# A sampling round's weighted sums, and what follows them, stand one round later in program order

## The chip, the cores and the metric

The kernel runs on one core of a Trainium2 chip. The metric is the device time of one execution in microseconds (us); the median of three executions before the change is 7738.43 us. All arithmetic is in float32.

## The reference

The input is four images of 256 channels by 64 by 64 pixels. Each image goes through four layers in a row. The first one is the one that the change touches, cut here to that part:

```python
# L0, per image: y = leaky_relu(bn(conv1x1(normed x))); xp = inproj(y)
offset, mask = linear(depthwise3x3(y))            # 4 groups x 9 points per pixel
sg   = reference_grid + dilation_grid + offset    # where each point lies
samp = grid_sample(pad(xp), sg)                   # 4 neighbours, bilinear
dout = (samp * softmax(mask)).sum(points)         # 36 weighted points per pixel
x2   = bn(y + outproj(dout))
x2   = x2 * squeeze_excite(mean(x2))              # needs the whole image's mean
out  = y + fc2(leaky_relu(fc1(x2)))
# then L1 linear attention with 5x5 depthwise, L2 3x3 convolution with signed
# weights, L3 a non-local block with softmax; group norms stand between them
```

The sampling is a gather: every pixel needs 36 points of a table, at addresses that the data decide.

## The kernel before

**Sampling.** `sample(n, ssum)` (L556) samples image n in 293 rounds. A round covers 14 pixels (`RP`), which is 126 of the 128 partitions with 9 points each. Sixteen rounds make a block of 224 pixels; an image has 18 such blocks and one of five rounds. In a round:

- `gathered` (L596) issues four indirect DMAs on GpSimd's queue, one per group, into a tile `g` of which seven buffers exist (L598), and then eight small matmuls on TensorE (L607, "the sums") that multiply the gathered rows by the weights `wm` and add them into `acc`, a PSUM bank used in two halves of two rounds each. Two rounds (`UR`) make a unit.
- `weigh` (L585, VectorE, L591) prepares `wm` for four rounds (`WR`) at a time; two `wm` buffers exist.
- What follows a unit's sums is put into `later`, a table from round number to functions: `moved` (L610, ScalarE copies `acc` to `at`, L612), `turned` (L614, TensorE transposes `at` into `dp`, L617), `spread` (L619, ScalarE copies `dp` into the block's `dT`, L632; of `dT` one buffer exists). After a block's last unit come, for each half of the output channels, `project` (L636, TensorE, L640), `add` (L642, VectorE, L644) and `finish` (L646, ScalarE, L649). At the start of each round, what `later` holds for it is issued (L658).
- `load` (L572) fetches the next block's table addresses and weights into `sl`, from the first round of a block.

**Side work.** The sampling loop is a generator. After each round, `beside` (L1194) advances the programs that run beside it by a portion of their steps: beside image 0 it is the first convolution of the other images and the sampling coordinates; beside image n it is the feed-forward of image n-1, then the linear attention of image n-1, and layers 2 and 3 of image n-2. After image 3's sampling a stretch without sampling finishes the last images.

**Order.** Under `manual_schedule`, TensorE, VectorE, ScalarE and GpSimd execute in the order in which the program issues their instructions. Only the Sync engine's DMA queue is arranged by the framework. GpSimd has, while the sampling goes on, nothing but gathers. So the place of a sampling step is its place among the portions of side work on its own engine:

```python
for f in later.pop(i, ()): f()      # start of round i
...gathered(sl, wm, acc, r)...      # four gathers, eight matmuls
yield 1                             # beside() issues portion i of the side work
```

Before the change, TensorE's order is thus: later(i), sums(i), portion(i), later(i+1), sums(i+1), portion(i+1), and so on.

Of the kernel before, what the change touches and what calls it, by code (L numbers as in the profile page):

```python
# [17 lines left out]
P = 128  # L18
N, C, H, W = 4, 256, 64, 64
HW = H * W  # L20
KT = C // P
# [8 lines left out]
RP, WR, UR, BR = 14, 4, 2, 16  # L30
RS, BP = RP * PT, RP * BR
BLOCKS = [(p0, min(BP, HW - p0)) for p0 in range(0, HW, BP)]
OB = 16
TY, TX = H + 2, W + 3
LEADS = 12, 14, 16, 18
SLOPE = 0.01

# [34 lines left out]
class Net:  # L72
# [483 lines left out]
    def sample(self, n, ssum):  # L556

        nc, sp = self.nc, self.sp
        table = self.tab[n].rearrange("g y x s c -> (g y x) (s c)")
        blocks, images, at, dp, dT, po, later = {}, {}, {}, {}, {}, {}, {}

        def halves(name):

            t = self.ps1.tile([P, 2, 256], F32, name=name, tag=name)
            return cycle([t[:, 0], t[:, 1]])

        accs, dps = halves("acc"), halves("dp")  # L570

        def load(b):  # L572
            p0, np_ = BLOCKS[b]
            whole, part = np_ // RP, np_ % RP

            nr = whole + (part > 0)
            sl = sp.tile([P, BR, G * 5], F32, name="sl")
            rows = self.s_d[n][p0 * PT:p0 * PT + nr * RS, :].rearrange("(r p) f -> p r f", p=RS)
            more = self.s_d[n][p0 * PT + RS:p0 * PT + (nr + 1) * RS, :].rearrange("(r p) f -> p r f", p=RS)
            nc.sync.dma_start(sl[0:RS, 0:nr], rows)  # L580
            nc.sync.dma_start(sl[RS:P, 0:nr], more[0:P - RS])
            rounds = [(r, RP) for r in range(whole)] + [(whole, part)] * (part > 0)
            blocks[b] = sl, rounds

        def weigh(b, r):  # L585

            sl, rounds = blocks[b]
            nu = min(WR, len(rounds) - r)
            wm = self.gp.tile([P, WR, 4 * G, OB], F32, name="wm")
            sh = [P, nu, 4 * G, OB]  # L590
            nc.vector.tensor_tensor(  # L591
                wm[:, 0:nu], self.con("own").unsqueeze(1).unsqueeze(1).to_broadcast(sh),
                sl[:, r:r + nu, G:].unsqueeze(3).to_broadcast(sh), ALU.mult)
            return wm

        def gathered(sl, wm, acc, r):  # L596
            r4, acc = r % WR, acc[:, r % UR * P:(r % UR + 1) * P]
            g = self.gp.tile([P, G, 256], F32, name="g", bufs=7)  # L598
            for i in range(G):
                nc.gpsimd.indirect_dma_start(  # L600
                    out=g[:, i, :], out_offset=None, in_=table,
                    in_offset=bass.IndirectOffsetOnAxis(ap=sl.bitcast(I32)[:, r, i:i + 1], axis=0))


            for x in range(2):
                for i in range(G):
                    nc.tensor.matmul(acc[32 * i:32 * i + 32, :], wm[:, r4, 4 * i + 2 * x:4 * i + 2 * x + 2, :],  # L607
                                     g[:, i, x * P:(x + 1) * P], start=x == 0, stop=x == 1)

        def moved(acc, nu, u):  # L610
            at[u] = sp.tile([P, UR, P], F32, name="at")
            nc.scalar.copy(at[u].rearrange("p v c -> p (v c)")[:, 0:nu * P], acc[:, 0:nu * P])  # L612

        def turned(nu, u):  # L614
            dp[u] = next(dps).rearrange("p (v g s o) -> p v g s o", v=UR, g=G, s=2)
            for v in range(nu):
                nc.tensor.transpose(dp[u][:, v].rearrange("p g s o -> p (g s o)"), at[u][:, v], self.ident)  # L617

        def spread(unit, b, u):  # L619

            if b not in dT:
                p0, np_ = BLOCKS[b]
                dT[b] = sp.tile([P, G, BP], F32, name="dT", bufs=1)
                images[b] = sp.tile([P, KT, BP], F32, name="yb")
                nc.sync.dma_start(images[b][:, :, 0:np_], self.y_d[n][:, :, p0:p0 + np_])
            full = sum(1 for _, m in unit if m == RP)
            for v0, v1, m in ((0, full, RP), (full, len(unit), unit[-1][1])):
                for s in range(2):
                    if v0 < v1:
                        hs = slice(64 * s, 64 * s + 64)  # L630
                        q0 = RP * (unit[0][0] + v0)
                        nc.scalar.copy(  # L632
                            dT[b][hs, :, q0:q0 + m * (v1 - v0)].rearrange("p g (v o) -> p g v o", o=m),
                            dp[u][hs, v0:v1, :, s, 0:m].rearrange("p v g o -> p g v o"))

        def project(b, m):  # L636
            np_ = BLOCKS[b][1]
            po[m] = self.ps("po")
            for k in range(G):
                nc.tensor.matmul(po[m][:, 0:np_], self.ow[:, k, m * P:(m + 1) * P], dT[b][:, k, 0:np_], start=k == 0, stop=k == G - 1)  # L640

        def add(b, m):  # L642
            ym = images[b][:, m, 0:BLOCKS[b][1]]
            nc.vector.tensor_tensor(ym, po[m][:, 0:BLOCKS[b][1]], ym, ALU.add)  # L644

        def finish(b, m):  # L646
            p0, np_ = BLOCKS[b]
            ym = images[b][:, m, 0:np_]
            nc.scalar.activation(ym, ym, AF.Identity, bias=self.sh[:, 4 + m:5 + m],  # L649
                                 scale=self.inv[:, 4 + m:5 + m], accum_out=ssum[:, m, b:b + 1])  # L650
            if m == KT - 1:
                nc.sync.dma_start(self.x2_d[n][:, :, p0:p0 + np_], images[b][:, :, 0:np_])

        load(0)
        order = [(b, r) for b, (_, np_) in enumerate(BLOCKS) for r in range(-(-np_ // RP))]
        wm = weigh(0, 0)
        for i, (b, r) in enumerate(order):
            for f in later.pop(i, ()):  # L658
                f()
            sl, rounds = blocks[b]  # L660
            if r % UR == 0:
                acc = next(accs)
            gathered(sl, wm, acc, r)
            if r == 0 and b + 1 < len(BLOCKS):
                load(b + 1)
            ends = r + 1 == len(rounds)
            if r % WR == 0:
                if r + WR < len(rounds):
                    nxt = weigh(b, r + WR)
                elif b + 1 < len(BLOCKS):  # L670
                    nxt = weigh(b + 1, 0)
            if r % UR == UR - 1 or ends:
                unit = rounds[r - r % UR:r + 1]
                todo = [partial(moved, acc, len(unit), i), partial(turned, len(unit), i), partial(spread, unit, b, i)]

                todo = [(i + 1 + j + (j == 2 and r < UR), f) for j, f in enumerate(todo)]
                if ends:
                    todo += [(i + 4 + m + j, partial(f, b, m)) for m in range(KT) for j, f in enumerate((project, add, finish))]
                for j, f in todo:
                    later.setdefault(j, []).append(f)  # L680
            if r % WR == WR - 1 or ends:
                wm = nxt
            yield 1
        for i in sorted(later):
            for f in later[i]:
                f()
# [73 lines left out]
    def layer1(self, n, st, st2):  # L760
# [3 lines left out]
        with tc.tile_pool(name=f"la{n}", bufs=1, side="right") as sp, \  # L764
# [17 lines left out]
            def step(cost, chains=False):  # L782
# [6 lines left out]
                if chains:  # L789
                    if count % 8 == 6 if self.alone else count in LEADS:  # L790
                        next(made, None)
# [551 lines left out]
```

## Time and profile before

| | |
|---|---|
| three executions | 7737.99, 7738.43, 7746.72 us |
| profiled execution, first to last instruction (the only time that its record gives) | 8805.8 us |
| first gather starts, last gather starts | 134.1 us, 7306.6 us |
| from there to the end | about 1,498 us |
| GpSimd: gathers, mean of one | 4,688, 985 ns |
| TensorE busy, granted clock, over the whole span | 68%, 0.81 |
| VectorE, ScalarE, GpSimd busy | 59%, 25%, 59% |

The profile is of one execution, which took 8805.8 us from its first to its last instruction; that is 13.8% more than the median of the three that were timed without a profile. It is read by stage: the sampling from 134 to 7,308 us, and the stretch without sampling after it. In the rows, "A <- B" names the tile that an instruction writes and the tiles that it reads; the last column is the time for which the engine stood idle before such instructions, and what ended most of that idle time. "issue" is time in which the engine waited for nothing that the profile shows, "remote" is a wait whose releaser the profile could not name.

### The profile page before, as it was taken

Reading aid. Unit: us, or ns where it says so; the run is one execution under the profiler, and the core shown is the slowest. Engines: PE = TensorE matmul, PEld = TensorE weight load, DVE = VectorE, ACT = ScalarE, POOL = GpSimd, SP = SyncE. Lnnn points to the kernel's source line nnn. Section 1 sums busy time; section 2 is a strip of 40 time slices with the busy share of each in tenths; the row PEclk is TensorE's granted clock in tenths of the full one; section 3 lists DMA queues with packets and bytes.
Section 4 is the critical chain, followed back from the end, with each engine's and each line's share of the span. In section 5 each row is a group of like instructions: output and inputs, shape, how many; then the busy total and the mean of one; then the engine's idle time right before and its main releaser. Section 6 shows DMA issues by size and latency. Waiting matters only on the chain. (4 is left out here: it accounts for less than half of the span.)

```text
span 8805.8 us, 95736 instructions
## 1 busy us (share of the span) xinstructions
PE 5993.9 (68%) x36532; PEld 3575.6 (41%) x36532; DVE 5173.3 (59%) x6409; ACT 2183.8 (25%) x4899; POOL 5152.4 (59%) x4950
## 2 busy tenths in 40 slices
PE   4454554448744446688876677888766778986899
PEld 2222222224323322244544443345544433664477
DVE  5444443443466667424777776227777772599834
ACT  1111111112211112122223222222222222465524
POOL 2666666566666666666666656666666661376410
PEclk7676766669866667799988888898878888998999
DMA  6454454444433334444443344444434343220131
GB/s 172 127 155 124 141 154 118 125 145 145 153 105 105 110 105 129 127 130 138 134 135 110 112 121 136 142 134 132 136 115 117 114 118 99 69 74 29 48 98 53
DMA packets 759050, 1042.27 MB, mean 118 GB/s; under 512 B 362432, under 2 KB 472128, under 8 KB 757056
## 3 DMA queue, kind: packets, MB, share of 16 engines
q0 software_dynamic: 225024, 614.77, 24.3%
q1 hardware_dynamic: 533568, 421.39, 16.4%
q8 instruction: 289, 4.73, 0.2%
q14 instruction: 169, 1.38, 0.0%
HBM read 867.08 MB, written 168.69 MB: 118 GB/s over the span
## 5 line engine op out<-in xcount | busy, mean ns | idle before, releaser
L600 POOL DMA_INDIRECT g<-tab,sl x4688 | 4618.5, 985 | 2687.8 <-issue 1224.2
L178 DVE SCALAR_TENSOR_TENSOR agg<-pad,vec,agg 128x1024 f32<-128x1024 f32 x2280 | 2933.5, 1287 | 61.9
L607 PE MATMUL acc<-g,wm 128*32 128x128 f32 x18752 | 1034.8, 333 | 1907.8 <-ACT at L612 1273.7
L607 PEld LDWEIGHTS acc<-g,wm 128*32 128x32 f32 x18752 | 566.8, 128 | 2411.7 <-ACT at L612 1446.1
L1048 PE MATMUL ps<-xd,w 128*128 128x256 f32 x3072 | 752.7, 396 | 51.3 <-issue 37.8
L591 DVE TENSOR_TENSOR wm<-con,sl 128x1024 f32<-128x1024 f32 (+1 forms) x296 | 357.7, 1209 | 711.9 <-remote 533.5
L1048 PEld LDWEIGHTS ps<-xd,w 128*128 128x128 f32 x3072 | 595.1, 199 | 175.0 <-issue 86.0
L632 ACT COPY dT<-dp 64x112 f32<-64x112 f32 x1176 | 285.9, 243 | 1043.7 <-remote 544.3
L742 PE MATMUL ps<-x2f,f 128*128 128x512 f32 x1024 | 499.2, 636 | 19.1 <-issue 7.7
L817 PE MATMUL ps<-xr,qw 128*128 128x512 f32 x768 | 472.0, 746 | 22.1 <-issue 11.1
L727 DVE SCALAR_TENSOR_TENSOR hm<-ps,vec,lk 128x512 f32<-128x512 f32 x256 | 190.8, 750 | 492.9 <-ACT lk L744 405.5
L752 PE MATMUL ps<-hm,f 128*128 128x512 f32 x1024 | 467.1, 605 | 0.9 <-DVE hm L727 0.9
L612 ACT COPY at<-acc 128x256 f32<-128x256 f32 (+1 forms) x588 | 218.3, 371 | 986.3 <-remote 753.2
L999 POOL TENSOR_TENSOR xd<-xp 128x640 f32<-128x640 f32 x64 | 79.4, 1268 | 492.6 <-ACT xp L1011 298.3
L640 PE MATMUL po<-dT,ow 128*128 128x224 f32 (+1 forms) x1216 | 326.1, 419 | 45.4 <-issue 19.3
L617 PE MATMUL dp<-ident,at 128*128 128x128 f32 x1172 | 284.1, 330 | 106.6 <-ACT dT L632 61.0
L865 ACT COPY kt<-pt 128x512 f32<-128x512 f32 x256 | 149.4, 584 | 829.3 <-remote 403.8
L744 ACT ACTIVATE lk<-ps,low 128x512 f32<-128x512 f32 x256 | 174.0, 687 | 666.0 <-PE ps L742 512.1
L1147 PE MATMUL s<-ph,th 128*128 128x512 f32 x512 | 290.2, 672 | 62.5 <-ACT kt L865 15.9
L640 PEld LDWEIGHTS po<-dT,ow 128*128 128x128 f32 x1216 | 265.5, 233 | 113.8 <-issue 68.9
L1167 PEld LDWEIGHTS ps<-gt,pT 128*128 128x128 f32 x2048 | 276.0, 213 | 70.8 <-issue 46.1
L194 POOL TENSOR_TENSOR ak<-ak,m 128x1024 f32<-128x1024 f32 x96 | 228.1, 2376 | 130.6 <-ACT m L193 126.7
(243 smaller groups left out, 8022.0 us busy)
## 6 DMA issues: line engine op xcount, KB each, us to landing
g<-tab,sl POOLq DMA_INDIRECT x4688
x<-x SPq DMA_DIRECT2D x128, 512.0 KB
xr<-x SPq DMA_DIRECT2D x96, 512.0 KB
tab<-xo SPq DMA_DIRECT2D x192, 128.0 KB
x<-in_x SPq DMA_DIRECT2D x32, 512.0 KB
y<-yc SPq DMA_DIRECT2D x32, 512.0 KB
x2f<-x SPq DMA_DIRECT2D x32, 512.0 KB
xyf<-x SPq DMA_DIRECT2D x32, 512.0 KB
```

What stands on the lines that cost most here:

```text
L178: nc.vector.scalar_tensor_tensor(to, s, wt, acc, ALU.mult, ALU.add)
L591: nc.vector.tensor_tensor(wm[:, 0:nu], self.con("own").unsqueeze(1).unsqueeze(1).to_broadcast(sh), sl[:, r:r + nu, G:].unsqueeze(3).to_bro ...
L600: nc.gpsimd.indirect_dma_start(out=g[:, i, :], out_offset=None, in_=table, in_offset=bass.IndirectOffsetOnAxis(ap=sl.bitcast(I32)[:, r, i: ...
L607: nc.tensor.matmul(acc[32 * i:32 * i + 32, :], wm[:, r4, 4 * i + 2 * x:4 * i + 2 * x + 2, :], g[:, i, x * P:(x + 1) * P], start=x == 0, st ...
L617: nc.tensor.transpose(dp[u][:, v].rearrange("p g s o -> p (g s o)"), at[u][:, v], self.ident)
L632: nc.scalar.copy(dT[b][hs, :, q0:q0 + m * (v1 - v0)].rearrange("p g (v o) -> p g v o", o=m), dp[u][hs, v0:v1, :, s, 0:m].rearrange("p v g ...
L640: nc.tensor.matmul(po[m][:, 0:np_], self.ow[:, k, m * P:(m + 1) * P], dT[b][:, k, 0:np_], start=k == 0, stop=k == G - 1)
L742: nc.tensor.matmul(ps, f1[:, k, m * P:(m + 1) * P], x2[:, k], start=k == 0, stop=k == KT - 1)
L752: nc.tensor.matmul(ps, f2[:, k, m * P:(m + 1) * P], hm[:, k], start=k == 0, stop=k == 4 * KT - 1)
L817: nc.tensor.matmul(ps, qw[:, k, m * P:(m + 1) * P], x[:, k], start=k == 0, stop=k == KT - 1)
L1048: nc.tensor.matmul(ps[:, e], w[:, k, t, 2 * half + e, m * P:(m + 1) * P], v[:, 2 * half + e, k, t:t + 8], start=i % 6 == 0, stop=i % 6 == 5)
L1147: nc.tensor.matmul(s[i], tv[:, 4 * b + j], ph[:, i * 512:(i + 1) * 512], start=True, stop=True)
```

## The change

A constant `LAG = 1` is added. `gathered` now only issues the four gathers; the eight matmuls become `weighted`, which is put into `later` for the next round. All that follows is put off by the same round: `moved`, `turned`, `spread`, `weigh`. Two distances grow by more than that. The `spread` of a block's first unit stands seven rounds after the unit's last round instead of four (the other units': four instead of three), and the projection begins seven rounds after the block's last round instead of four.

```diff
+LAG = 1
...
-        def gathered(sl, wm, acc, r):
-            r4, acc = r % WR, acc[:, r % UR * P:(r % UR + 1) * P]
+        def gathered(sl, r):
             g = self.gp.tile([P, G, 256], F32, name="g", bufs=7)
             for i in range(G):
                 nc.gpsimd.indirect_dma_start(
...
-
-
+            return g
+
+        def weighted(g, wm, acc, r):
+            r4, acc = r % WR, acc[:, r % UR * P:(r % UR + 1) * P]
             for x in range(2):
                 for i in range(G):
                     nc.tensor.matmul(acc[32 * i:32 * i + 32, :], wm[:, r4, 4 * i + 2 * x:4 * i + 2 * x + 2, :],
...
-            gathered(sl, wm, acc, r)
+            later.setdefault(i + LAG, []).append(partial(weighted, gathered(sl, r), wm, acc, r))
             if r == 0 and b + 1 < len(BLOCKS):
                 load(b + 1)
             ends = r + 1 == len(rounds)
-            if r % WR == 0:
-                if r + WR < len(rounds):
-                    nxt = weigh(b, r + WR)
+            if r % WR == LAG:
+                if r + WR - LAG < len(rounds):
+                    nxt = weigh(b, r + WR - LAG)
                 elif b + 1 < len(BLOCKS):
                     nxt = weigh(b + 1, 0)
...
-                todo = [(i + 1 + j + (j == 2 and r < UR), f) for j, f in enumerate(todo)]
+                todo = [(i + LAG + 1 + j + (j == 2 and r < UR) * 3, f) for j, f in enumerate(todo)]
                 if ends:
-                    todo += [(i + 4 + m + j, partial(f, b, m)) for m in range(KT) for j, f in enumerate((project, add, finish))]
+                    todo += [(i + LAG + 6 + m + j, partial(f, b, m)) for m in range(KT) for j, f in enumerate((project, add, finish))]
```

## The prediction

> **What bounds the kernel now.** I read the windows by stage first, then GpSimd's gathers: what they cost and what they wait for. The rows of the gathers and of the sums, from the list of the costliest groups:
>
> ```profile
> L600 POOL DMA_INDIRECT g<-tab,sl x4688 | 4618.5, 985 | 2687.8 <-issue 1224.2
> L607 PE MATMUL acc<-g,wm 128*32 128x128 f32 x18752 | 1034.8, 333 | 1907.8 <-ACT at L612 1273.7
> ```
>
> A gather holds GpSimd for 985 ns, and 4,007 of the 4,688 start 1224.2 / 4007 = 0.31 us after the one before with nothing to wait for. So GpSimd's own pace is 4618.5 + 4688 x 0.3055 = 6051 us for all rounds, 5.16 us a round. The gathers run from 134.1 to 7307.6 us, which is 7173.5 us; 1122 us of it are waits. The view of the gathers' line names them:
>
> ```profile
> its engine sat idle before it (us, times) until:
>   issue: 1224.2, 4007
>   remote: 624.7, 307
>   PE acc L607: 494.3, 201
> ```
>
> The second large one says that a gather waits for sums, that is for one of the seven `g` buffers. How far the sums are behind is seen by counting both in the same window (0 to 4,500 us; the number after x is the count), gathers first, sums second:
>
> ```profile
> 0.00:4500.00 4500.00, 2860.00 (x2886) 0.74 0.46 132
> ```
>
> ```profile
> 0.00:4500.00 4500.00, 667.00 (x11456) 361.44 (x11456) 0.74 0.46 132
> ```
>
> Four gathers make a round, and 18752 / 1172 = 16 matmul records: 2886 / 4 - 11456 / 16 = 721.5 - 716 = 5.5 rounds. To 3,000 us it is 1890 / 4 - 7472 / 16 = 5.5 too. So in the profiled execution TensorE is far behind: the data have been lying there for some five rounds when the sums come. What TensorE waits for at the sums is shown by their line and by a piece of the timeline:
>
> ```profile
> its engine sat idle before it (us, times) until:
>   ACT at L612: 2719.8, 588
> ...
>   DMA g<-tab,sl: 46.3, 49
> ```
>
> ```profile
> 3005.97 0.50 ACT L632 COPY dT<-dp 64x112 f32<-64x112 f32 x2
> 3006.49 0.37 ACT L612 COPY at<-acc 128x256 f32<-128x256 f32 x1
> 3006.91 1.08 PE L607 MATMUL acc<-g,wm 128*32 128x128 f32 x16 [6.59 <-ACT at L612]
> ```
>
> The first sums of a unit (588 units) start 0.05 us after ScalarE's copy of the unit before ended. ScalarE gets there only when it is through with its share of the side work. That handshake, not the landing of a gather (46.3 us in all), is where the profiled TensorE loses time.
>
> **The execution without a profile is bounded otherwise.** Were all 1122 us of waits gone, the profiled execution would be 8805.8 - 1122 = 7684 us. The median is 7738.4. If gathers and the stretch after them cost the same without a profile, which nothing here shows, only some 55 us of waits are left, 0.05 us a round: GpSimd's own pace is then the bound and TensorE keeps up. The "remote" waits (624.7 us at the gathers, none of weight after 7,345 us) speak for it: releases later than the recorded end of any work, in the stage with the most records. I take GpSimd as the bound. All sums below are against the 8805.8 us of the profile and are carried over to the median as differences.
>
> **What the Trainium skill says.** "Perfetto Trace Analysis", section "DMA Instruction — SWDGE (GPSIMD)": the end that the profiler gives for such a gather is the end of descriptor generation, not of the movement. The trace agrees: the last packet of a round's gathers ends a median 2.35 us after the fourth one's start, against 0.95 us for its row. So 985 ns is what occupies GpSimd, and the landing adds 2.35 us that only the first user could feel. "PSUM — Partial Sum Buffer", section "PSUM bank collisions raise a hardware error": guard PSUM by bank and quadrant, not by address. The two halves of `acc` share a bank, and the trace shows sums into one half waiting for the copy out of the other. The same page, "Engine vs sequencer instructions": the queues of ScalarE, VectorE and GpSimd are strictly first in, first out, and matmuls start and complete in program order. That fits the handshake above.
>
> **The change part by part.** No instruction is added or removed: 4,688 gathers, the same matmuls, copies and DMAs.
>
> *The shift.* Before: sums(i), portion(i), sums(i+1). After: portion(i), sums(i), portion(i+1). `moved`, `turned`, `weigh` and the rest go along on ScalarE and VectorE. Seen from these three engines, every portion is one round earlier relative to all sampling work, and each handshake keeps its neighbours: `moved` still stands directly ahead of the unit's first sums, with one portion between it and the sums that it copies; `weigh` still waits for sums one portion back. Cost by structure: 0. What it does alter is which portion meets which round; 588 handshakes of a mean 1273.7 / 588 = 2.2 us on TensorE are dealt anew. While GpSimd sets the pace this is covered by the seven `g` buffers (36 us of gathers); without that cover I bound it at -60 to +60 us, 5% of 1273.7.
>
> *The gathers.* Their order on GpSimd is the same, and nothing else is in that queue. Gather i+7 waits for sums(i), which now stand behind portion(i); but portion(i) no longer waits for gather i, only for i-1. Both ends of the slack move by one round: 0. If the sums had waited for landing data, up to 2.35 us a round would be hidden; 46.3 us of waits in all say that they don't.
>
> *Queues of DMAs.* The loads of `sl` are issued from the same round. In the trace they start 89 us or more ahead of a block's first gather, 26 to 28 us for the first block of images 1 to 3. The block's `yb` load and `x2` write move three rounds back, behind other transfers on SP; `yb` is needed about eight rounds later, so that covers it: 0.
>
> *The block's end.* The projection starts seven rounds after the block's last round instead of four; the `dT` copies of the next block's first unit move behind it, and the second unit's copies, which now come first into the one `dT` buffer, stand in the same round as the second half of the projection, directly ahead of a `moved`. So TensorE: projection, then ScalarE: two copies (2 x 0.243, row L632) and `at` (0.371), then TensorE: sums. That is 0.86 us a block in which TensorE has to wait, where before a round lay between. There are 76 - 4 = 72 such places: 62 us if TensorE sets the pace, 0 if GpSimd does. With 55 of 1122 us of waits left, 5% of 62: **+3 us**.
>
> *The image's end.* Portion 292 now precedes the last sums. After the last image that takes (4609.2 - 1034.8) / 1172 = 3.0 us of side work (TensorE's busy time from 134 to 7,308 us less the sums, per round) from behind the last landing, and adds one `at` copy and one group of sums in a row, 0.37 + 0.65 us. Bounds -3 to +2; I take **-2 us**. At the other three ends the next image's gathers run on and cover it.
>
> Sum: +3 - 2 = **+1 us**, 8807 in the profile, or 7739 on the median. I give 7742, since the redealing of handshakes can use up slack and can hardly create it where GpSimd is the bound.
>
> **Rivals.** *TensorE sets the pace (slower).* If gathers are faster without a profile than 1.25 us, waits for `g` buffers remain in number, and the handshake at each block's end is paid: 62 us, plus 3 x 1.0 us at image ends: about 7803. If the copy out of `acc` also no longer hides behind the projection (8 matmul records x 0.19 us = 1.5 us at full clock), 72 x 2.4 = 170 us: 7908 as the outer end. For it: 494.3 us of gathers waiting for sums. Against it: the 55 us. It decides once GpSimd waits for sums in most blocks for more than the 0.86 us.
>
> *The shift pays (faster).* If TensorE, unhindered by a profile, catches up with the gathers and has to wait for landing, side work now runs in that time. As GpSimd's order is untouched, it can gain at most the 55 us of waits that are left: floor 7683, its middle 7712.
>
> *The change doesn't do what it says.* "Behind the next round's gathers" orders two different queues; no engine has both. What it does is only the shift against the side work. That is my forecast.
>
> **How the numbers follow.** A measurement of this kernel can tell about 0.2% from no change, 15.5 us. GpSimd as the bound: 0.52, of it 0.43 within, 0.06 slower, 0.03 faster. TensorE sets the pace: 0.32, of it 0.02 within, 0.30 slower. Handshakes redealt or landing hidden with a net effect: 0.16, of it 0.10 faster, 0.01 within, 0.05 slower. Together faster 0.13, same 0.46, slower 0.41. The range goes from the faster rival's middle (7712) to half-way between the slower rival's two values (7803 and 7908), 7856; beyond lie about 0.06 below and 0.10 above.
>
> **What would show it.** Right: 4,688 gathers of 985 ns with the same 0.31 us between; `at` still the releaser of most idle time ahead of the sums; gathers 5 to 6 rounds ahead in a profiled execution; first to last gather within 1% of 7173 us. The block's end: idle time at `dT` L634 (now L632) that ends with the projection, some 70 times. Wrong: waits of the gathers for sums that grow by over 60 us (TensorE sets the pace), or fall by as much (the shift pays).

## The result: 0.5% slower, and the profile after

| | before | after |
|---|---|---|
| median (lowest to highest), 4 executions each | 7740.07 us (7737.99 to 7746.72) | 7779.76 us (7771.42 to 7789.07) |
| ratio, 95% interval | | 1.005 (1.0038 to 1.0061) |
| profiled execution, first to last instruction | 8805.8 us (e1: 7738.6) | 7769.6 us |
| waits of the gathers, over the usual 0.30 us between two | 1129.7 us (e1: 99.9) | 145.2 us |

The kernel after takes 40 us more. Its profile seems to say the opposite: 7769.6 us against 8805.8. The two profiles can't be set against each other. The same kernel before, profiled once more (run e1 below), spans 7738.6 us and was timed at 7740.4 us in that very execution, no longer than its executions without a profile (7733.44 to 7752.09 us), so the profiler adds nothing that can be seen. The 8805.8 us fit another chip: on the one that ran e12 the kernel before takes 8776.82 us (7 executions, 8763 to 8784). On which chip the first profile was taken isn't on record. From here on "before" is the profile of e1.

The rows of the gathers and of the sums, from the list of the costliest groups, first before (e1), then after:

```profile
L600 POOL DMA_INDIRECT g<-tab,sl x4688 | 4592.7, 980 | 1657.3 <-issue 1308.6
L607 PE MATMUL acc<-g,wm 128*32 128x128 f32 x18752 | 1321.2, 320 | 1103.9 <-DMA g<-tab,sl 553.3
```

```profile
L600 POOL DMA_INDIRECT g<-tab,sl x4688 | 4582.0, 977 | 1706.9 <-issue 1321.0
L609 PE MATMUL acc<-g,wm 128*32 128x128 f32 x18752 | 1324.4, 320 | 1211.1 <-ACT at L614 617.5
```

A gather costs the same (980 and 977 ns), a matmul of the sums too (320 ns). What grew is idle time: 50 us ahead of the gathers, 107 us ahead of the sums, and there the main releaser is now ScalarE's `at` copy where it was the landing of the gathered rows. The view of the gathers' line says what GpSimd waits for (us, times), before (e1) and after:

```profile
  issue: 1308.6, 4295
  DMA sl<-sd: 134.1, 1
  PE acc L607: 126.5, 109
```

```profile
  issue: 1321.0, 4335
  PE acc L609: 174.7, 118
  DMA sl<-sd: 135.9, 1
```

The wait for sums, that is for a free `g` buffer, grew by 48 us, in about as many places. From the first gather's start to the last one's end it is 135.4 to 6251.3 us before, 137.2 to 6290.2 after: 37 us more. The end after the last gather is 1487.3 against 1479.5 us. So the loss lies in the gathers' waits. Summed block by block, all that a gather stands idle over 0.30 us ahead of a round, in us:

| | image 0 | image 1 | image 2 | image 3 | blocks 14, 15, 16 of image 2 | of image 3 |
|---|---|---|---|---|---|---|
| before (e1) | 8.8 | 8.4 | 41.1 | 41.7 | 0.1, 9.2, 12.6 | 0.1, 11.7, 12.4 |
| after | 3.8 | 16.4 | 61.6 | 63.3 | 13.3, 25.5, 11.9 | 12.3, 25.6, 11.6 |

The growth is 45 us, and three blocks of eighteen, in two images, hold more than all of it (+29 and +25 us). GpSimd's waits for sums while TensorE does the sums of blocks 10 to 15 of image 2 (us, times, longest), from the list of waits, before (e1, 4025 to 4553 us) and after (4016 to 4572 us):

```profile
POOL g L600 <- PE acc L607: 22.6, 14, 4.3
```

```profile
POOL g L600 <- PE acc L609: 53.5, 20, 7.4
```

What can make the sums late is seen in the timeline. In block 14 of image 2 the same portion of side work (linear attention, layers 2 and 3) lies in both kernels behind other sums. After (columns: start, duration, engine, line, operation, in brackets the idle time ahead and its releaser):

```profile
4432.05 0.64 PE L609 MATMUL acc<-g,wm 128*32 128x128 f32 x16
...
4437.37 3.06 PE L819 MATMUL ps<-xr,qw 128*128 128x512 f32 x4 [1.82 <-DVE ot L918]
...
4440.47 0.78 ACT L829 ACTIVATE pad<-ps,g_add,vec 128x512 f32<-128x512 f32 x1 [6.09 <-PE ps L819]
...
4442.82 0.49 ACT L634 COPY dT<-dp 64x112 f32<-64x112 f32 x2
4443.33 0.37 ACT L614 COPY at<-acc 128x256 f32<-128x256 f32 x1
4443.75 0.63 PEld L609 LDWEIGHTS acc<-g,wm 128*32 128x32 f32 x16 [4.89 <-ACT at L614]
4443.75 1.08 PE L609 MATMUL acc<-g,wm 128*32 128x128 f32 x16 [3.32 <-ACT at L614]
```

Before (e1):

```profile
4431.10 3.78 PE L817 MATMUL ps<-xr,qw 128*128 128x512 f32 x4 [3.17 <-DVE ot L916]
...
4434.68 0.64 PE L617 MATMUL dp<-ident,at 128*128 128x128 f32 x2
4434.93 0.78 ACT L827 ACTIVATE pad<-ps,g_add,vec 128x512 f32<-128x512 f32 x1 [8.17 <-PE ps L817]
4435.24 0.63 PEld L607 LDWEIGHTS acc<-g,wm 128*32 128x32 f32 x16 [0.33 <-DMA g<-tab,sl]
4435.24 0.92 PE L607 MATMUL acc<-g,wm 128*32 128x128 f32 x16
```

In both, TensorE ends its share of the portion with the four matmuls into `ps`, and ScalarE only then begins its own: `pad`, then the exponentials `pe`. After, the next sums are the first of a unit. They wait until ScalarE has done all of it and then copied the unit before out of the shared bank: 3.32 us in which TensorE has nothing. Before, the next sums are the second round of a unit, which need no copy: they start while ScalarE is at `pad`. A unit is two rounds. If heavy portions come on rounds of one parity, a shift by one round moves them from ahead of second rounds to ahead of first ones. That reading is what the experiments had to test.

This is one place, and it doesn't speak for its block. Summed over stretches, TensorE's waits for the `at` copy ahead of the sums of image 2 are these (us, times, longest), over the sums of blocks 8 to 13, before (e1, 3856.8 to 4347.9 us) and after (3847 to 4353.8 us):

```profile
PE acc L607 <- ACT at L612: 62.7, 29, 6.8
PE acc L609 <- ACT at L614: 89.1, 36, 10.3
```

And over the sums of blocks 14 to 16, before (4347.9 to 4628.9 us) and after (4353.8 to 4643.1 us):

```profile
PE acc L607 <- ACT at L612: 30.4, 14, 5.2
PE acc L609 <- ACT at L614: 26.5, 18, 5.3
```

So this wait grew by 26 us ahead of block 14, where free buffers hid it, and it shrank a little in the three blocks in which GpSimd then has to stand. The sums of blocks 8 to 13 take 506.8 us instead of 491.0, longer by three rounds of 5.16 us, and the gathers are six rounds ahead instead of three when the sums of block 14 begin. In blocks 14 to 16 the sums take 289.3 us instead of 281.1; these 8 us come of other waits, since TensorE's busy time is 231 us in both. Image 3 shows the same. The loss appears in blocks 14 to 16 and is for the larger part made before them.

### The profile page after: what moved, and what is told of

Same layout as the page of the kernel before. It is cut to its first block, busy times and chain, and to the rows that moved or that the text cites. A ratio compares the mean times of both kernels' runs of the same rounds, so it can differ in the third digit from the quotient of the medians.

```text
span 7769.6 us, 95692 instructions
## 1 busy us (share of the span) xinstructions
PE 5993.6 (77%) x36532; PEld 3529.5 (45%) x36532; DVE 5159.1 (66%) x6409; ACT 2190.7 (28%) x4899; POOL 5114.8 (66%) x4950
## 5 line engine op out<-in xcount | busy, mean ns | idle before, releaser
L609 PE MATMUL acc<-g,wm 128*32 128x128 f32 x18752 | 1324.4, 320 | 1211.1 <-ACT at L614 617.5
L609 PEld LDWEIGHTS acc<-g,wm 128*32 128x32 f32 x18752 | 646.8, 121 | 1918.8 <-ACT at L614 839.4
L1050 PE MATMUL ps<-xd,w 128*128 128x256 f32 x3072 | 706.9, 382 | 7.0 <-DVE x L1030 3.4
L1050 PEld LDWEIGHTS ps<-xd,w 128*128 128x128 f32 x3072 | 573.4, 191 | 106.0 <-issue 30.3
L744 PE MATMUL ps<-x2f,f 128*128 128x512 f32 x1024 | 480.4, 617 | 4.0 <-ACT f L719 4.0
L819 PE MATMUL ps<-xr,qw 128*128 128x512 f32 x768 | 452.0, 720 | 7.5 <-DVE ot L918 3.6
L642 PE MATMUL po<-dT,ow 128*128 128x224 f32 (+1 forms) x1216 | 299.1, 396 | 32.3 <-DVE yb L646 10.5
L744 PEld LDWEIGHTS ps<-x2f,f 128*128 128x128 f32 x1024 | 191.3, 195 | 232.0 <-issue 218.2
L1169 PE MATMUL ps<-gt,pT 128*128 128x128 f32 x2048 | 288.6, 300 | 7.0 <-ACT pT L1165 6.8
```

What stands on the lines that cost most here:

```text
L744: nc.tensor.matmul(ps, f1[:, k, m * P:(m + 1) * P], x2[:, k], start=k == 0, stop=k == KT - 1)
L819: nc.tensor.matmul(ps, qw[:, k, m * P:(m + 1) * P], x[:, k], start=k == 0, stop=k == KT - 1)
L1050: nc.tensor.matmul(ps[:, e], w[:, k, t, 2 * half + e, m * P:(m + 1) * P], v[:, 2 * half + e, k, t:t + 8], start=i % 6 == 0, stop=i % 6 == 5)
L1169: nc.tensor.matmul(ps[:, 0:P], pT[:, m], gt[:, m], start=m == 0, stop=m == 7)
```

## Experiments

Times are medians; each ratio is to the kernel before on the same chip, with its 95% interval. Waits are the gathers' idle time over 0.30 us a round. In the edits, `LAG` is the distance of the sums from their gathers, and two more constants stand for the 3 and the 6 of the changed `todo` lines: `FIRST` and `PROJECT`. The kernel before has `LAG, FIRST, PROJECT = 0, 1, 4`, the kernel after `1, 3, 6`.

**e1: the kernel before once more, unaltered.**

> The kernel before, unchanged, for a second profile of it. Both theories hold that the execution without a profile is bound by GpSimd's gathers with few waits, so a profile that runs as the timed executions do must show a span near 7738 us, first to last gather within 100 us of 6051 us, and waits ahead of the gathers of under 150 us in all instead of 1122. Theory A (the changed places at a block's end and the redealt portions cost time where TensorE is tight) expects about 40 us less of these waits than the 145 us of the changed kernel, in the same few blocks of images 2 and 3. Theory B (the sums come later, so g buffers come free later) expects the difference spread over all images. Theory C (the end: what follows the last gather) expects equal waits and a stretch after the last gather some 40 us shorter than the 1479 us of the changed kernel. If the span is near 8800 us again, the first profile was no accident.

Measured: 7743.33 us, 1.0002 (0.9993 to 1.0011), profiled span 7738.6 us, waits 99.9 us. No wait of weight is named "remote" at the gathers, where the first profile had 624.7 us.

**e2: the gathers alone.** Distances as before, and the portions one round later, so that TensorE, VectorE and ScalarE have the order of the kernel before; what remains of the change is that gathers are issued one round earlier against them.

```diff
-LAG = 1
+LAG, FIRST, PROJECT = 1, 1, 4
-                advance(i / number)
+                advance(min(1, max(0, (i + -1) / number)))
```

> Lag 1 with the distances of before, and every portion of side work one round later, so that the order of TensorE, ScalarE and VectorE is that of before: only the gathers are issued one round ahead of it. Theory A: no difference to before, within 0.1% (7740 us), since GpSimd has nothing but gathers in its queue. Theory B: slower, by most of the 40 us, since what is ahead of the sums in program order is the same as in the change.

Measured: 7773.41 us, 1.0042 (1.0028 to 1.0056), waits 121.2 us. TensorE's wait for `at` ahead of the sums is that of before (521.1 us in all, e1 521.2). In the profile 7 us of the excess stand behind the last gather (1494.2 us against 1487.3): portions that come a round later are left over at the end of an image.

**e3: the order alone.** No lag, but the distances of the kernel after and the portions one round earlier: the order of the kernel after on these three engines.

```diff
-LAG = 1
+LAG, FIRST, PROJECT = 0, 3, 6
-            later.setdefault(i + LAG, []).append(partial(weighted, gathered(sl, r), wm, acc, r))
+            weighted(gathered(sl, r), wm, acc, r)
-                advance(i / number)
+                advance(min(1, max(0, (i + 1) / number)))
```

> No lag (sums in the round of their gathers), but the longer distances to the spread and to the projection, and every portion of side work one round earlier: the order of TensorE, ScalarE and VectorE is that of the changed kernel. Theory A: as slow as the changed kernel, about +40 us (7780). Theory B: as fast as before (7740), since no sums wait a round.

Measured: 7778.4 us, 1.005 (1.0036 to 1.0063), waits 143.9 us, in blocks 14 to 16 as after (13.3, 25.5, 11.9 in image 2). Its wait for `at` is also that of after (625.9 us in all, after 617.5). So the order alone is enough for the whole loss and for its pattern. That e2 also loses 32 us doesn't fit this: its blocks 14 to 16 are as before (0.1, 11.7, 12.6), and the excess in its gathers' waits lies in the first blocks of images 1 to 3. The two effects don't add up in the kernel after, and this part stays open.

**e4: the extra distances taken back, the lag kept.**

```diff
-LAG = 1
+LAG, FIRST, PROJECT = 1, 0, 3
```

> The changed kernel with the projection four rounds after the block's last round as before (now seven) and the first unit's spread in its ordinary place. It is theory A split: if the places at a block's end cost the 40 us, it runs as before or faster (7730 to 7745 us); if the redealt portions do, or the lag itself (theory B), it stays near 7780 us.

Measured: 7759.55 us, 1.0027 (1.0019 to 1.0034), waits 117.4 us (blocks 14 to 16 of image 2: 0.3, 22.9, 14.9). About half of the loss hangs on where the projection and the first `spread` stand (the latter now three rounds after its unit, one less than before the change). The expected 7730 to 7745 us didn't come, nor did 7780. It could be their wait for each other, or again which portion comes ahead of what.

**e5 and e6: one `g` buffer fewer**, in the kernel before and in the kernel after.

```diff
-            g = self.gp.tile([P, G, 256], F32, name="g", bufs=7)
+            g = self.gp.tile([P, G, 256], F32, name="g", bufs=6)
```

> The kernel before with six g buffers instead of seven. The waits ahead of the gathers stand in few blocks of images 2 and 3 (blocks 1 to 4, and 14 to 16), where TensorE's round takes longer than GpSimd's 5.16 us and the buffers run full. If buffers are the reserve that such a stretch uses up, one fewer costs one round, 5 us, for each of the some five stretches: about +25 us (7765). If the waits are single late sums instead, all rounds with TensorE 5 behind would wait: well over +100 us.

> The changed kernel with six g buffers. Reserve: about +25 us on the changed kernel as well, so some 7805 us, and the distance to the kernel before with six stays near 40 us. It is the base for the next run.

Measured: 7759.77 us, 1.0028 (1.0019 to 1.0037), and 7799.6 us, 1.0079 (1.0062 to 1.0095). One buffer, 5.16 us of cover, is worth some 20 us in either kernel. The cover is thus used up in both, at several places in each.

**e7: e6 with two `dT` buffers**, which takes away ScalarE's wait for the projection.

```diff
-                dT[b] = sp.tile([P, G, BP], F32, name="dT", bufs=1)
+                dT[b] = sp.tile([P, G, BP], F32, name="dT", bufs=2)
```

> The changed kernel with six g buffers and two dT buffers: the spread to a new block no longer waits for the projection of the last (411 us of ScalarE's idle time in 66 places, 45 us in 26 in the kernel before). Theory A1 (this wait of ScalarE, with all that stands behind it in its queue, is what the change costs): back to the level of the kernel before with six buffers, some 30 to 40 us below the changed kernel with six. Theory A2 (the redealt portions and the first unit's late spread cost it): within 8 us of the changed kernel with six.

The view of the `dT` copies' line, what ScalarE waits for there (us, times), after and then e7:

```profile
  PE dp L619: 616.9, 143
  PE po L642: 411.4, 66
```

```profile
  PE dp L619: 822.4, 186
```

The 66 waits for the projection (`po`) are gone. The time is 7790.53 us, 1.0065 (1.0048 to 1.0082), beside e6's 7799.6: 9 us by the medians, with intervals that overlap. That is near A2's bound of 8 us and far from A1's 30 to 40. A wait of 6.2 us (411.4 / 66) on ScalarE is dear only where somebody stands behind it; most of these hold up nobody.

**e8 and e9: the kernel before, only dealt anew.** The portions of side work come one round later, or two. Nothing else differs, but that what is left of them at an image's end comes behind its last sums; the stretch after the last gather is 10 us longer in both (1497.7 and 1496.8 us).

```diff
-                advance(i / number)
+                advance(min(1, max(0, (i + -1) / number)))   # e9: i + -2
```

> The kernel before, with every portion of side work one round later and nothing else: only the dealing of portions to rounds is changed, in the other direction than the change does it. Theory A2: the dealing is worth tens of us either way, so some 10 to 40 us off 7740. Theory A1: within 10 us of 7740, but for one round of side work at each image's end.

> The kernel before, with every portion of side work two rounds later. Theory P (parity): what a portion costs depends on whether the round after it begins a unit. There TensorE waits for the copy out of acc, which stands behind the portion on ScalarE; in the second round of a unit it doesn't. One round of displacement, in either direction, swaps the two kinds of rounds under the heavy portions of blocks 14 to 16 (one round later: 7805 us); two rounds give the old kind back, so the waits in these blocks return to the 22 to 24 us an image of the kernel before, and the time to 7740 to 7760 us. Theory D (any displacement costs by its length or by chance): 7800 us or more.

The gathers' wait for sums (us, times), e8 and then e9:

```profile
  PE acc L609: 187.7, 130
```

```profile
  PE acc L609: 111.0, 99
```

Measured: e8 7805.3 us, 1.0081 (1.0064 to 1.0098); e9 7743.26 us, 1.0004 (0.9995 to 1.0012). One round costs 65 us with none of the change in it, more than the 10 to 40 us expected; two rounds cost nothing. The gathers' waits in blocks 14 to 16 of image 2 go the same way: 43 us in e8, 25 in e9, 22 before. That is what parity against the two-round unit expects. It isn't all that matters, since e2 loses 32 us with the order kept. Nor do these two runs show that the price is paid at the handshake: over the sums of blocks 8 to 13 of image 2 TensorE waits 72.5 us for `at` in e8 and 74.3 us in e9, which are alike, and in blocks 14 to 16 it waits 26.9 and 24.6 us. Through which waits e8 loses stays open.

**e10 and e11: the handshake taken away.** The halves of `acc` go into two PSUM banks, each beside a half of `dp`; e10 is the kernel before with this edit, e11 the kernel after. Ahead of the sums TensorE and its weight loads wait for the `at` copy 1249.4 us in 670 places in e1, 2.7 us in 3 places in e10, and nowhere in e11.

```diff
-        def halves(name):
-            t = self.ps1.tile([P, 2, 256], F32, name=name, tag=name)
-            return cycle([t[:, 0], t[:, 1]])
-        accs, dps = halves("acc"), halves("dp")
+        one, two = (self.ps1.tile([P, 2, 256], F32, name=name, tag=name) for name in ("acc", "dp"))
+        accs, dps = cycle([one[:, 0], two[:, 0]]), cycle([two[:, 1], one[:, 1]])
```

> The kernel before, with the two halves of acc in two PSUM banks and dp in their other halves, so that the first sums of a unit no longer wait for the copy of the unit before; the transpose waits for it one round later. Theory P: this takes the price of parity away; the waits ahead of the gathers in blocks 14 to 16 shrink, and the time falls to about 7700 us (7690 to 7730). Theory D: within 10 us of 7740.

> The changed kernel with the same two banks. Theory P: without the wait at a unit's first sums the change has nothing to cost, so it runs within 12 us of the kernel before with two banks. Theory D: it stays some 40 us above that.

The gathers' line in e10 (L596; the sums go by two tile names now):

```profile
L596 POOL DMA_INDIRECT g<-tab,sl x4688: 942/947/2025, 138.6 to 6181.0; - x196
...
  issue: 1327.6, 4357
  DMA sl<-sd: 137.3, 1
  DMA g<-tab,sl: 55.4, 169
  PE acc L603: 14.3, 26
  PE dp L603: 10.9, 26
```

Measured: e10 7665.07 us, 0.9898 (0.9881 to 0.9914); e11 7663.22 us, 0.9902 (0.9887 to 0.9917). Both are faster than theory P expected (7690 to 7730 us). Waits for sums fall to 25.2 us in e10, the sampling lasts 6043 us, and the two kernels are alike to 2 us. With the handshake goes the whole difference of the change in the time, and the kernel before gains 75 us. That all of the loss was paid at the handshake doesn't follow. Without it the sums are only two rounds behind when block 14 begins, in either kernel, so that the buffers cover other delays too. Such a delay is there: in e11 the sums of block 15 of image 2 take 101.6 us, in e10 88.9, with no handshake in either, and the gathers wait 13.4 us in blocks 15 and 16, in e10 0.2. Either one, about 1.0% faster than before, is the best version found.

**e12: e2 with two banks.**

> The kernel of e2_gathers_early (order of the sums as before, gathers one round earlier), with the halves of acc and dp in two PSUM banks as in e10. Theory P (a portion ahead of a unit's first sums delays them through ScalarE's copy of the unit before; two banks take that handshake away): what e2 lost against the kernel before (7773.41 against about 7740 us, +32) goes too, and it comes within 12 us of e10's 7665.07: 7653 to 7677. Rival Q (e2's loss comes of gathers that run earlier at the start of each image, through the landing of their rows or the buffers of the slots, and has nothing to do with the unit's handshake): some 30 us stay: 7690 to 7705.

Measured: 8710.98 us, on a chip where the kernel before takes 8776.82 us (8763.31 to 8784.35, 7 executions): 0.9923 (0.9907 to 0.994). Carried over to 7740 us that would be 7668 to 7694, which meets both expectations, and the comparison with e10 is across two chips. So whether e2's 32 us come through the unit's handshake is not settled. The gathers' line of e12:

```profile
  issue: 1252.0, 4095
  remote: 619.0, 281
  PE acc L605: 221.8, 66
  PE dp L605: 182.7, 72
```

They are much like those of the first profile of the kernel before (1224.2, 624.7 and 494.3 us), on a chip that runs at this speed with no profiler too.

## Why the prediction was right or wrong

The range held the time; the likeliest case, within 0.2% of before, didn't come. The time went to the slower side, by 40 us where +1 was summed up. That the range held it is in part luck: its upper half is there for the slower rival, and what that rival describes isn't what happened. Step by step:

- **GpSimd as the bound: right for these chips, for a wrong reason.** The prediction took the 1122 us of waits as due to the profiled execution, and the "remote" ones as a sign of it. Waits like these, "remote" ones too, come in e12 on a chip on which every execution is about so long, without a profiler too; there the gathers wait in every block. That the profile might be of another chip was not among the cases weighed. On the chips that were timed, GpSimd's own pace was 6043 us where its waits are nearly gone (e10); 6051 had been worked out.
- **"Only some 55 us of waits left": measured 99.9.** The size was near. What failed was to spread it: "0.05 us a round" is a mean over 1,172 rounds, while 46 of the 83 us of images 2 and 3 lie in blocks 15 and 16.
- **The redealing of handshakes, "covered by the seven `g` buffers": this is the step that failed.** It was taken as 0; e3 shows that the order, with the longer distances, makes the whole 40 us, and e4 that 19 us stay when the distances are short. The bound without cover, -60 to +60 us, would have held it. In blocks 14 and 15 of image 2 the sums of sixteen rounds took 110.3 and 94.4 us before, against 16 x 5.16 = 82.6 of GpSimd's pace: 28 and 12 us too long, where seven buffers cover at most 36 us and three of them were in use when block 14 began. After it is 115.2 and 102.6 us, and six are in use at the start, since the handshakes of blocks 8 to 13 cost 26 us more and the sums of these blocks take 16 us longer. e5 and e6 show the missing cover, e8 that redealing alone costs, e10 and e11 that without the handshake the loss is gone. In the sentence "each handshake keeps its neighbours" the flaw is plain: the neighbours among the sampling steps stay, the portion behind which `at` stands doesn't.
- **"If the sums had waited for landing data": 0 came, but not by the figure given.** The 46.3 us of waits for landing rows are of the profile of 8805.8 us. The sums' line, before (e1) and after, shows TensorE and its weight loads waiting for them throughout, as the prediction's faster rival supposed:

```profile
  DMA g<-tab,sl: 1388.9, 1556
  ACT at L612: 1249.4, 670
```

```profile
  ACT at L614: 1456.9, 782
  DMA g<-tab,sl: 1420.4, 1583
```

  The shift hides none of it: the sums catch up with the gathers in images 0 and 1 (median one round behind) in either order, and whoever has caught up waits at the gathers' pace. So the faster rival was right about the landing and wrong about the gain; its own ground, that GpSimd's order is untouched, spoke against it.
- **The block's end, +3 us.** The waits at `dT` for the projection came as foreseen, 66 for some 70. They are 6.2 us each on ScalarE (the 0.86 us were TensorE's share), and taking them away is worth some 9 us of the time (e7). e4 puts half of the loss on the distances at the block's end, so +3 us was too low; whether that half is the same dealing no run showed.
- **The image's end, -2 us.** The stretch after the last gather is 7.8 us shorter after. But e3, with the same order, has 1491.6 us there and before 1487.3, so this is within what one profile differs from another.
- **The loads of `sl`, 0.** In the prediction's trace one of them starts 73 us ahead of its block (block 10 of image 0), not 89 or more. No gather but the very first waits for one, so the 0 stands.
- **The slower rival** gave 7803 for a TensorE that sets the pace everywhere. It does so only in some of the first blocks of images 1 to 3 and in blocks 14 to 16 of images 2 and 3. The price is the unit's handshake at least as much as the block's end. The gathers' waits grew by 45 us, below the 60 set as the mark.

The Trainium skill's sentence in "PSUM — Partial Sum Buffer", section "PSUM bank collisions raise a hardware error", that PSUM has to be guarded by bank and not by address, bore the explanation: under such a guard the two halves of `acc` in one bank are no double buffer between TensorE and ScalarE. The traces agree, with 670 waits for the copy out of the other half in e1 and 3 with two banks (e10), and the runs add the price, 75 us of 7740.

## What to carry to other kernels

Slack is not a mean: before a stall is called covered, look for the stretch in which the buffers are already full, count the cover there, and look ahead of it for what used the cover up. When a change shifts a periodic job against another one, ask which parity meets which wait; shifting only the side work by one and by two steps, with all else kept, tells in two runs whether it matters, though not through which wait. One place in a timeline shows how a wait comes about; only the sum over stretches shows where it grew. And try the two buffers of a producer and a consumer on different engines in two PSUM banks; here that was the largest gain.

## What the runs showed of the hardware that was not expected

The kernel before took 7740 us on the chips of the other experiments and 8777 us on the one of e12, within 0.2% each. Whether that is the chip's nature or a state that it was in, no run shows. In e12's profile TensorE's granted clock is 0.807 on average (0.848 in e1), 5% lower, and a gather takes 987 ns (980), which doesn't explain 13%. The sign is another one: gathers are a median five to six rounds ahead of the sums, and still TensorE and its weight loads stand idle 2,038 us ahead of the sums in 2,894 places (0.70 us each) for nothing that the profile names. In e10, with the same banks on a chip of the usual speed, such time is 329 us in 886 places, the sums in images 0 and 1 run one round behind the gathers, and what they wait for is the landing. Why TensorE goes on late on the other chip no run shows. The kernel with two banks was faster there too: e12, with e2's edit in it, by 0.8%.
